# Five loads of x, statistics ahead of the first search, and another constant under the unread products, in a two-layer graph-and-expert kernel

## The chip, the cores and the metric

The kernel runs on one core of a Trainium2 chip, as one program launched once. The metric is the device time of that program in microseconds (us). Engines are named as in the profile: PE (matrix products; PEld is its weight loads), DVE (vector), ACT (scalar, activations), POOL (general), SP (here it only issues transfers). All five run their own instructions in order and wait for each other by semaphores. A name with a q behind it (SPq, ACTq, POOLq) is an engine's issue of DMA transfers.

## The reference

Two layers, each a graph step and an expert step, on x of 2708 x 256 in float32. Only the first layer's front is touched by the change:

```python
# layer 0, graph step: adj holds values up to 1e9, so each row's softmax is decided by its largest entry
h = layernorm(x) @ weight
logits = h @ conv_weight1 + (h @ conv_weight2).T
coefs = softmax(leaky_relu(logits) + adj, axis=-1)
x = x + coefs @ h + bias
# layer 0, expert step: layernorm, rmsnorm, causal attention with rotary positions, router, 8 experts, top 2
x = x + ffn0(layernorm(x))
# layer 1
x = x + sigmoid(masked_softmax_attention(layernorm(x), adj != 0))
x = x + ffn1(layernorm(x))
```

## The kernel before

The 2708 rows are 22 tiles of 128 rows (the last has 20). The function `first` does layer 0 up to the attention and the first experts' blocks. It doesn't multiply by the softmax: for each row it searches the adjacency's row for its largest entry (`top`, a MAX8, L974), finds where it is (`index`, L978), and fetches that row of h from memory with an indirect transfer that adds it into x (`fetch`, L996). The safety of that (the gap between the two largest entries and so on) is tested at the end by a flag.

**The planner.** `first` does not write its instructions in a fixed order. Each piece of work is a step given to a `Plan` (L74 to L146) with an engine, an assumed length in us, the steps it needs, buffers that it takes and gives back, a rank (lower goes first), and for a transfer a time `lands` between its issue and its data. `issue` plays this through on paper: at each turn it takes, of the steps that can start soonest, the one of the lowest rank, and emits its instructions. The emitted order is what each engine then runs. So the order is fixed when the program is built, from assumed lengths, and on the chip an engine whose next instruction is not ready waits, whatever stands behind it. Where the plan has a gap of over 1 us on PE, `fill` puts products nobody reads into it (0.75 x gap / 0.24 of them; each is two matmul records in the profile), which multiply the constant `allones` with the constant `before` (L1267).

**The steps around the change**, in the order in which a tile goes through them:

- the loads of x on SP: tiles 0 to 3, tiles 4 to 20, and the last tile (L834 to L839). Each has the rank -9; `lands` grows with the number of tiles.
- `rest` (ACT): transfers of the bias row, the routers and the second layer's graph weight; `wg_in`, a step without instructions, stands for the landing of the first layer's graph weight, whose transfer is issued before the plan starts (L184).
- `centre` (L866): PE multiplies the weight by ones to get column sums (L872), DVE takes the mean off (L876). It is done once for the graph weight (rank -3, result `wgc`) and once for the attention's `wq_sb` (rank -0.5), after `load_wq` (SP) and `order_wq` (ACT, L855 and L858).
- `project(t0)` for each pair of tiles, rank -1: `stats` (DVE, L267, L269, L897) and `power` (POOL, L901) give each row's scale; `turn` (PE, L908, rank -2) transposes x; `back` (ACT, L917) brings that from PSUM; `times` (PE, L928) multiplies by `wgc`, into one of two PSUM banks in turn; `out_` (ACT, L935) scales by `rsx` and frees the bank; `store` (ACT's queue, L940) writes the pair's h to `hd` in memory; `bias` (POOL, L912) adds the bias to x.
- `tile_in(t)` for each of the 22 tiles, rank t: `load` (SP, L969 the adjacency's 128 rows, 1354 KB, into one of three slots; L971 the rotary table), `top` and `index` (DVE, rank t + 2), `narrow` (ACT, L988, a bf16 copy of the adjacency in two halves; needs the last pair's `store`) and `save` (SP, L991), which frees the slot for tile t + 3; `fetch` (POOL, needs `index`, `bias` and every pair's `store`); then statistics, norm, transposes, the products for q, k, v and the rotary step.
- `pair(t0)`: the attention of two tiles of queries, on PE (L1100, L1126), ACT (L1106) and DVE (L1145), needs `tile_in` of all tiles up to t0 + 1.

Behind `first` follow the experts of layer 0, the second layer and its experts; all of it hangs on what is in front.

The constant `before` is made by POOL (an iota) and then by DVE (L231) in the preamble; `allones` by POOL alone (L228).

Of the kernel before, what the change touches and what calls it, by code (L numbers as in the profile page):

```python
# [17 lines left out]
PE, SP = mybir.EngineType.PE, mybir.EngineType.SP  # L18
PSUM = bass.MemoryType.PSUM

P = 128
N = 2708
C = 256
KC = C // P
NT = (N + P - 1) // P
# [40 lines left out]
def rows(t):  # L66
    return min(P, N - t * P)
# [6 lines left out]
class Plan:  # L74
# [16 lines left out]
    def add(self, engine, length, run, needs=(), take=(), give=(), rank=0.0, lands=0.0):  # L91
        step = dict(engine=engine, length=length, run=run, needs=[n for n in needs if n is not None],
                    take=take, give=give, rank=rank, lands=lands, end=None)
        self.steps.append(step)
        return step
# [54 lines left out]
def adj_ffn_kernel(ctx, tc, x, adj, vecs, bias_rows, tab, w_gnn0, w_gnn1, wqkv, wo,  # L150
                   r0, r1, w1_0, w3_0, w2_0, w1_1, w3_1, w2_1, out):
    nc = tc.nc
# [59 lines left out]
    def ramp(name, shape, pattern, base=0, mult=0):  # L212
        t = const.tile(shape, F32, name=name)
        nc.gpsimd.iota(t, pattern=pattern, base=base, channel_multiplier=mult,
                       allow_small_or_imprecise_dtypes=True)
        return t
# [10 lines left out]
    allones = const.tile([P, P], F32, name="allones")  # L227
    nc.gpsimd.memset(allones, 1.0)  # L228

    before = ramp("before", [P, P], [[1, P]], 0, -1)  # L230
# [34 lines left out]
    def moments(src, r):  # L265
        st = small.tile([P, nc.vector.BN_STATS_DIM], F32, tag="st", name="st")
        nc.vector.bn_stats(out=st[:r], in_=src)  # L267
        mv = small.tile([P, nc.vector.BN_AGGR_DIM], F32, tag="mv", name="mv")
        nc.vector.bn_aggr(out=mv[:r], in_=st[:r])  # L269
        return mv  # L270
# [517 lines left out]
    def first(X, XB, norms, tops, hd, mb, xs, acc, arena, load_weights):  # L788
# [11 lines left out]
        with ExitStack() as s:  # L800
# [29 lines left out]
            add = plan.add  # L830


            loads = []
            for a, b in ((0, 4), (4, NT - 1)):  # L834
                loads.append(add("SP", 0.5, lambda a=a, b=b: nc.sync.dma_start(
                    out=X[:, a:b, :], in_=x[a * P:b * P, :].rearrange("(t p) c -> p t c", p=P)),
                    rank=-9.0, lands=1.5 + 0.4 * (b - a)))
            loads.append(add("SP", 0.5, lambda: nc.sync.dma_start(
                out=X[:rows(NT - 1), NT - 1, :], in_=x[(NT - 1) * P:N, :]), rank=-9.0, lands=9.0))  # L839
            rest = add("ACT", 2.0, load_rest, rank=-9.0, lands=8.0)  # L840


# [17 lines left out]
            a = add("SP", 1.2, load_wq, loads, take=["e"], rank=1.5, lands=3.0)  # L860
# [5 lines left out]
            def centre(out_w, w, wide, needs, rank):  # L866
                v = {}

                def total():
                    v["p"] = mm_tile()  # L870
                    for k in range(KC):
                        nc.tensor.matmul(v["p"][:, :wide], allones, w[:, k, :], start=(k == 0), stop=(k == KC - 1))  # L872

                def less():
                    for k in range(KC):
                        nc.vector.scalar_tensor_tensor(out_w[:, k, :], v["p"][:, :wide], -1.0 / C, w[:, k, :],  # L876
                                                       ALU.mult, ALU.add)

                a = add("PE", wide / 256, total, needs, take=["mm"], rank=rank)
                return add("DVE", wide / 340, less, [a], give=["mm"], rank=rank)  # L880

            wg_in = add("SP", 0.0, lambda: None, rank=-9.0, lands=3.0)
            centred = centre(wgc, wg[0], C, [wg_in], -3.0), centre(wq_sb, wq_sb, 2 * C, [wq_in], -0.5)

            stored, biased = [], []
# [2 lines left out]
            def project(t0):  # L888
                two = [t0, t0 + 1]
                v = {}  # L890
                rank = -1.0
                bank = ("o", "zs")[t0 // 2 % 2]

                def stats(t):
                    r = rows(t)
                    v["mv", t], v["pv", t] = moments(X[:r, t, :], r), small.tile([P, 1], F32, tag="pv", name="pv")
                    nc.vector.tensor_scalar(v["pv", t][:r], v["mv", t][:r, 1:2], 1.0, 1e-5, ALU.mult, ALU.add)  # L897

                def power(t):
                    r = rows(t)  # L900
                    nc.gpsimd.tensor_tensor(out=rsx[:r, t:t + 1], in0=v["pv", t][:r], in1=mhalf[:r, 0:1], op=ALU.pow)  # L901

                def turn():
                    v["pt"] = tr_tile()
                    for i, t in enumerate(two):
                        r = rows(t)
                        for k in range(KC):
                            nc.tensor.transpose(v["pt"][:, i * KC + k, :r], X[:r, t, k * P:(k + 1) * P], ident[:r, :r])  # L908

                def bias(t):  # L910
                    r = rows(t)
                    nc.gpsimd.tensor_tensor(out=X[:r, t, :], in0=X[:r, t, :], in1=brow[:r, 0, :], op=ALU.add)  # L912

                def back():
                    v["xT"] = ab.tile([P, 2, NREP, P], F32, tag="yT", name="xTt").rearrange("p a b c -> p (a b) c")
                    if rows(t0 + 1) == P:
                        nc.scalar.copy(v["xT"], v["pt"])  # L917
                    else:
                        for i, t in enumerate(two):
                            nc.scalar.copy(v["xT"][:, i * KC:(i + 1) * KC, :rows(t)],  # L920
                                           v["pt"][:, i * KC:(i + 1) * KC, :rows(t)])

                def times():
                    v["po"] = afp.tile([P, 2 * W2], F32, tag=bank, name="po")
                    for i, t in enumerate(two):
                        r = rows(t)
                        for k in range(KC):
                            nc.tensor.matmul(v["po"][:r, i * C:(i + 1) * C], v["xT"][:, i * KC + k, :r], wgc[:, k, :],  # L928
                                             start=(k == 0), stop=(k == KC - 1))

                def out_():
                    v["hs"] = ab.tile([P, 2 * W2], F32, tag="osb", name="hs").rearrange("p (t c) -> p t c", t=2)
                    for i, t in enumerate(two):
                        r = rows(t)
                        nc.scalar.activation(v["hs"][:r, i, :], v["po"][:r, i * C:(i + 1) * C], AF.Copy,  # L935
                                             scale=rsx[:r, t:t + 1])

                def store():
                    if rows(t0 + 1) == P:
                        nc.scalar.dma_start(out=hd[t0 * P:(t0 + 2) * P, :].rearrange("(t p) c -> p t c", p=P),  # L940
                                            in_=v["hs"])
                    else:
                        for i, t in enumerate(two):
                            nc.scalar.dma_start(out=hd[t * P:t * P + rows(t), :], in_=v["hs"][:rows(t), i, :])

                x_in = [loads[0]] if t0 < 4 else [loads[1]] if t0 + 2 < NT else loads[1:]
                s_ = {t: add("DVE", 0.85, lambda t=t: stats(t), x_in, take=["mv"], rank=rank) for t in two}
                c = [add("POOL", 0.6, lambda t=t: power(t), [s_[t]], give=["mv"], rank=rank) for t in two]
                a = add("PE", 0.5, turn, x_in, take=["mm"], rank=rank - 1.0)
                for t in two:  # L950
                    biased.append(add("POOL", 0.8, lambda t=t: bias(t), [a, s_[t], rest], rank=rank + 1.5 + t / NT))
                a = add("ACT", 0.6, back, [a], take=["yT"], give=["mm"], rank=rank - 1.0)
                a = add("PE", 1.75, times, [a, centred[0]], take=[bank], give=["yT"], rank=rank)
                a = add("ACT", 0.95, out_, [a] + c, take=["ob"], give=[bank], rank=rank)
                stored.append(add("ACT", 0.35, store, [a], give=["ob"], rank=rank, lands=2.5))
# [285 lines left out]
            a = None  # L1241
            weights = []
            for e in range(2):
                a = add("SP", 6.0, lambda e=e: load_weights(e), cleared + [a], rank=NT + 3.0 + e, lands=3.0,
                        take=[] if e else [f"{a}{i}" for i in range(3) for a in ("adj", "low")])
# [17 lines left out]
            def idle(bank, pool):  # L1263
                def run(n):
                    nobody = pool.tile([P, 2 * W2], F32, tag=bank, name="nobody")
                    for _ in range(n):
                        nc.tensor.matmul(nobody[:, :P], allones, before, start=True, stop=True)  # L1267
                return run

            plan.fillers = [("zs", 1, idle("zs", afp)), ("o", 1, idle("o", afp))]  # L1270
# [1122 lines left out]
```

## Time and profile before

| what | us |
|---|---|
| three timed runs | 1506.54, 1506.64, 1509.68 (median 1506.64) |
| the profiled execution, its own time | 1506.29 |
| span of its records | 1504.5 |
| PE busy in the span | 1417.7 (94%) |
| DVE, ACT, POOL busy | 762.5, 567.4, 529.9 |
| third x load issued, then the first, second and third adjacency load | 5.51, 6.30, 9.61, 18.42 |
| first and last `times` begin (PE, L928; the last 8 of 16 records that run from 46.54 for 3.72) | 16.83, 48.4 |
| first `fetch` (POOL, L996) | 53.78 |
| fourth adjacency load issued | 57.28 |

The profile's page gives busy shares over the span, a strip of 40 slices, the costliest groups and the chain of waits that ended last. The trace behind it can be asked for the instructions of a stretch in order of time (a row is: start, duration, engine, line, operation, output tile and inputs, count, and in brackets how long the engine idled before and what released it) and for busy times in given stretches.

### The profile page before, as it was taken

The page shows a single profiled execution, that of the slowest core. Times are in us where ns is not written, and L with a number is a line of the kernel's source. Part 1 is how long each engine was busy: PE and PEld are TensorE (multiplying, and loading weights), DVE is VectorE, ACT ScalarE, POOL GpSimd, SP SyncE. Part 2 cuts the span into 40 slices and gives each one's busy share as a digit, 9 for nine tenths or more (in the row PEclk, how much of TensorE's full clock was granted, in tenths as well). Part 3 has the DMA queues.
Part 4 walks back from the last instruction along what each step waited for, and adds up shares of the span by engine and source line. Part 5 has one row for each costly group of instructions (what it writes and reads, how often), then busy time and mean ns, then how long its engine had stood idle before and what let it go on. Part 6 is the DMA issues. An engine that isn't in the chain of part 4 may idle for free. (4 is left out here: it accounts for less than half of the span.)

```text
span 1504.5 us, 21112 instructions
## 1 busy us (share of the span) xinstructions
PE 1417.7 (94%) x7488; PEld 1030.2 (68%) x7488; DVE 762.5 (51%) x1647; ACT 567.4 (38%) x1134; POOL 529.9 (35%) x681
## 2 busy tenths in 40 slices
PE   5878989989999999999999989999999999999995
PEld 5633433433335888888888778888769878888884
DVE  5688999966676322222222564766745322222221
ACT  2576776755554322222221443444323212122220
POOL 5577668782152221222222310030434122222222
PEclk9999999999999999999999999999999999999998
DMA  7599757430011666656411860633412965566111
GB/s 261 190 298 291 256 193 235 146 121 8 7 41 42 172 194 176 182 150 185 113 15 22 183 133 1 137 80 98 154 48 75 273 190 140 160 173 169 15 18 20
DMA packets 198519, 201.83 MB, mean 134 GB/s; under 512 B 93248, under 2 KB 168520, under 8 KB 195696
## 3 DMA queue, kind: packets, MB, share of 16 engines
q1 hardware_dynamic: 173782, 170.96, 37.4%
q0 software_dynamic: 20352, 25.85, 9.7%
q10 hardware_dynamic: 4270, 3.58, 0.7%
q8 instruction: 61, 1.00, 0.3%
q14 instruction: 54, 0.44, 0.1%
HBM read 128.46 MB, written 56.37 MB: 123 GB/s over the span
## 5 line engine op out<-in xcount | busy, mean ns | idle before, releaser
L2065 PE MATMUL pup<-xTs,arena 128*128 128x256 f32 (+2 forms) x1320 | 252.8, 350 | 0.6 <-ACT xTs L2048 0.6
L2065 PEld LDWEIGHTS pup<-xTs,arena 128*128 128x128 f32 (+1 forms) x1320 | 219.5, 190 | 28.3 <-PE y L2130 2.3
L1582 PE MATMUL po<-hb,PT 128*128 128x257 f32 (+2 forms) x968 | 228.5, 390 | 4.0 <-DVE PT L1575 4.0
L2069 ACT ACTIVATE sl<-pup 128x256 f32<-128x256 f32 (+1 forms) x210 | 73.6, 350 | 370.8 <-PE pup L2065 369.1
L1582 PEld LDWEIGHTS po<-hb,PT 128*128 128x128 f32 (+2 forms) x968 | 177.3, 189 | 44.0 <-issue 13.1
L2070 DVE TENSOR_TENSOR hT<-sl,pup 128x256 f32<-128x256 f32 (+1 forms) x210 | 79.6, 379 | 229.0 <-ACT sl L2069 228.7
L1106 ACT ACTIVATE e<-stt 128x1024 f32<-128x1024 f32 (+1 forms) x132 | 125.4, 986 | 93.6 <-PE stt L1100 68.5
L617 POOL DMA_INDIRECT out<-ys,XR x45 | 69.4, 1542 | 246.7 <-DVE ys L2083 110.0
L1145 DVE TENSOR_TENSOR es<-es,e 128x1024 f32<-128x1024 f32 x104 | 138.0, 1327 | 29.8 <-ACT e L1106 23.1
L617 POOL DMA_INDIRECT acc<-ys,XR x45 | 69.8, 1552 | 226.3 <-DVE ys L2083 94.5
L1100 PE MATMUL stt<-qT,kT 64*128 64x512 f32 (+1 forms) x528 | 132.6, 612 | 6.3 <-ACT e L1106 6.1
L2080 PE MATMUL y<-arena,hT 128*128 128x256 f32 x612 | 136.7, 379 | 0.0
L1809 POOL DMA_INDIRECT xs<-XR,place x88 | 93.4, 1061 | 92.8 <-DVE mk L1569 41.3
L2080 PEld LDWEIGHTS y<-arena,hT 128*128 128x128 f32 x612 | 114.3, 190 | 14.5
L1126 PE MATMUL o<-e,V 128*64 128x512 f32 (+1 forms) x528 | 123.3, 590 | 0.0
L1560 ACT ACTIVATE E<-sb,dcol 128x768 f32<-128x768 f32 (+1 forms) x88 | 75.1, 859 | 108.5 <-DVE PT L1575 108.2
L2083 DVE TENSOR_SCALAR ys<-y,XR 128x256 f32<-128x256 f32 x71 | 34.3, 484 | 141.2 <-PE y L2080 141.1
L2065 PE MATMUL pup<-xTs,room 128*128 128x256 f32 (+3 forms) x528 | 99.9, 346 | 0.0
L1100 PEld LDWEIGHTS stt<-qT,kT 64*128 64x128 f32 x528 | 44.4, 187 | 78.1 <-issue 61.7
L2065 PEld LDWEIGHTS pup<-xTs,room 128*128 128x128 f32 (+1 forms) x528 | 85.4, 189 | 9.8 <-PE y L2130 0.8
L1126 PEld LDWEIGHTS o<-e,V 128*64 128x64 f32 x528 | 33.2, 137 | 69.9 <-issue 55.4
L974 DVE MAX8 tops<-arena 128x8 f32<-128x2708 f32 (+1 forms) x22 | 65.3, 2970 | 1.8 <-DMA arena<-in_adj 1.8
(316 smaller groups left out, 2026.0 us busy)
## 6 DMA issues: line engine op xcount, KB each, us to landing
more<-in_w SPq DMA_DIRECT2D x60, 640.0 KB
arena<-in_adj SPq DMA_DIRECT2D x21, 1354.0 KB
arena<-in_w SPq DMA_DIRECT2D x36, 640.0 KB
mb<-mb SPq DMA_DIRECT2D x44, 352.0 KB
XR<-xs SPq DMA_DIRECT2D x80, 134.0 KB
xs<-none SPq DMA_DIRECT2D x16, 536.0 KB
room<-in_w SPq DMA_DIRECT2D x12, 640.0 KB
acc<-X SPq DMA_DIRECT2D x21, 128.0 KB
```

The costliest lines, as they stand in the source:

```text
L617: nc.gpsimd.indirect_dma_start(out=acc[:, :], out_offset=bass.IndirectOffsetOnAxis(ap=tokens.bitcast(I32), axis=0), in_=ys, in_offset=None ...
L1100: nc.tensor.matmul(st[:r, g, c0(sb):], kT[a:b, sb * P:sb * P + r], qT[a:b, t0 + (sb == t0 + 1):t0 + 2, :, :], start=True, stop=True)
L1106: nc.scalar.activation(e[:r, :, c0(sb):], v[sb, "st"][:r, :, c0(sb):], AF.Exp, scale=1.0 / HD ** 0.5)
L1126: nc.tensor.matmul(v["o"][g * HD:(g + 1) * HD, c:], V[:r, sb, g * HD:(g + 1) * HD], v[sb][:r, g, c:], start=(n + i == 0), stop=(n + i == t ...
L1145: nc.vector.tensor_tensor(es, es, v[sb][:r, :, c:], ALU.add)
L1560: nc.scalar.activation(e[:q, :n], sb[:q, i0:i1], AF.Exp, bias=dcol[:q, j:j + 1], scale=SLOPE - 1.0)
L1582: nc.tensor.matmul(v["po", i][:r, :F], v["PT", j][:q, a:a + r], hb[:q, j, :], start=(j == 0), stop=(j == NT - 1))
L1809: i = nc.gpsimd.indirect_dma_start(out=xs[:, :], out_offset=bass.IndirectOffsetOnAxis(ap=at, axis=0), in_=src, in_offset=None)
L2065: nc.tensor.matmul(pp[:to, i, :B, :], wn[:, c, :], xT[:, c, :B, :], start=(c == 0), stop=(c == KC - 1))
L2069: nc.scalar.activation(sl[:, :B, :], pp[:, 0, :B, :], AF.Silu)
L2070: nc.vector.tensor_tensor(hT[:, n, :B, :], sl[:, :B, :], pp[:, 1, :B, :], ALU.mult)
L2080: nc.tensor.matmul(y, hT[:, n, b, :], w[3][:, n, :], start=(n == 0), stop=(n == NHC - 1))
```

## The change

- x is loaded by six transfers in place of three: tiles 0 to 3, 4 to 7, 8 to 11, 12 to 15, 16 to 20, and the last. The planner's assumed time on SP is 0.55 us a tile (it was 0.5 us a transfer), and each lands 2.2 us later.
- `stats` of a tile and `turn` of a pair need the piece that holds them, where tiles 4 to 20 had one load for all.
- `turn` of every pair from the third on needs the centred weight `wgc`.
- `wg_in` becomes a step of ACT with rank -10 (it was on SP) and lands at 4.0.
- The unread products multiply `allones` with itself in place of `before`.

```diff
             loads = []
-            for a, b in ((0, 4), (4, NT - 1)):
-                loads.append(add("SP", 0.5, lambda a=a, b=b: nc.sync.dma_start(
+            ends = (4, 8, 12, 16, NT - 1, NT)
+            for a, b in zip((0,) + ends, ends[:-1]):
+                loads.append(add("SP", 0.55 * (b - a), lambda a=a, b=b: nc.sync.dma_start(
                     out=X[:, a:b, :], in_=x[a * P:b * P, :].rearrange("(t p) c -> p t c", p=P)),
-                    rank=-9.0, lands=1.5 + 0.4 * (b - a)))
-            loads.append(add("SP", 0.5, lambda: nc.sync.dma_start(
-                out=X[:rows(NT - 1), NT - 1, :], in_=x[(NT - 1) * P:N, :]), rank=-9.0, lands=9.0))
+                    rank=-9.0, lands=2.2))
+            loads.append(add("SP", 0.3, lambda: nc.sync.dma_start(
+                out=X[:rows(NT - 1), NT - 1, :], in_=x[(NT - 1) * P:N, :]), rank=-9.0, lands=2.2))
...
-            wg_in = add("SP", 0.0, lambda: None, rank=-9.0, lands=3.0)
+            wg_in = add("ACT", 0.0, lambda: None, rank=-10.0, lands=4.0)
...
-                x_in = [loads[0]] if t0 < 4 else [loads[1]] if t0 + 2 < NT else loads[1:]
-                s_ = {t: add("DVE", 0.85, lambda t=t: stats(t), x_in, take=["mv"], rank=rank) for t in two}
+                x_in = [loads[sum(t >= e for e in ends)] for t in two]
+                s_ = {t: add("DVE", 0.85, lambda t=t: stats(t), x_in[t - t0:t - t0 + 1], take=["mv"], rank=rank) for t in two}
                 c = [add("POOL", 0.6, lambda t=t: power(t), [s_[t]], give=["mv"], rank=rank) for t in two]
-                a = add("PE", 0.5, turn, x_in, take=["mm"], rank=rank - 1.0)
+
+                a = add("PE", 0.5, turn, x_in + [centred[0]] * (t0 > 2), take=["mm"], rank=rank - 1.0)
...
-                        nc.tensor.matmul(nobody[:, :P], allones, before, start=True, stop=True)
+                        nc.tensor.matmul(nobody[:, :P], allones, allones, start=True, stop=True)
```

## The prediction

> **What bounds the kernel now.** The page's own chain of waits covers the last 17 us alone, so I went by stages: first the busy times in stretches, then the instructions of the first 70 us in order of time, then SP's waits behind that. The stretches (us, PE, PEld, DVE, ACT, POOL busy, PE's granted clock, DMA share, GB/s):
>
> ```profile
> 0.00:57.00 57.00, 40.33 (x205) 34.29 (x206) 36.61 (x98) 21.38 (x45) 33.04 (x73) 0.91 0.60 204
> 57.00:160.00 103.00, 84.49 (x393) 40.64 (x393) 85.98 (x86) 73.04 (x134) 73.98 (x109) 0.97 0.88 286
> 160.00:310.00 150.00, 136.68 (x616) 58.55 (x617) 144.41 (x169) 104.11 (x182) 109.89 (x137) 0.99 0.65 210
> ...
> 15.00:27.00 12.00, 11.09 (x66) 9.72 (x65) 8.48 (x25) 3.41 (x8) 5.84 (x11) 1.00 1.03 360
> 27.00:55.00 28.00, 21.89 (x100) 17.46 (x101) 21.58 (x45) 14.01 (x34) 18.88 (x31) 0.85 0.30 107
> ```
>
> From 57 us on the tile loop keeps DVE and the transfers nearly full, then DVE and PE. Before it lies a prologue in which nothing is full, and from 27 to 55 us the transfers are at 0.30: three adjacency slots are loaded and the fourth waits. Why, the order of time shows:
>
> ```profile
> 9.14 0.22 DVE L231 TENSOR_SCALAR before<-before 128x128 f32<-128x128 f32 x1
> 9.41 4.22 PE L1267 MATMUL nobody<-before,allones 128*128 128x128 f32 x22 [9.41 <-DVE before L231]
> 13.47 1.04 PE L908 MATMUL pm<-ident,X 128*128 128x128 f32 x8
> 14.74 1.13 PE L872 MATMUL pm<-wg,allones 128*128 128x256 f32 x4 [0.24 <-ACT xTt L917]
> ...
> 16.83 1.89 PE L928 MATMUL po<-wgc,xTt 128*128 128x256 f32 x8
> ...
> 18.43 2.98 DVE L974 MAX8 tops<-arena 128x8 f32<-128x2708 f32 x1 [1.76 <-DMA arena<-in_adj]
> ...
> 21.33 0.41 DVE L267 BATCH_NORM_STATS2 st<-X 128x6 f32<-128x256 f32 x1
> ...
> 30.98 0.84 ACT L935 ACTIVATE hs<-po,rsx 128x256 f32<-128x256 f32 x2 [6.87 <-POOL rsx L901]
> ...
> 31.87 3.78 PE L928 MATMUL po<-wgc,xTt 128*128 128x256 f32 x8 [5.78 <-ACT hs L935]
> ```
>
> ```profile
> 50.85 0.99 ACTq L944 DMA_DIRECT2D hd<-hs  x2
> ...
> 53.78 1.79 POOL L996 DMA_INDIRECT X<-hd,ix  x1 [8.32 <-issue]
> ...
> 54.24 2.55 ACT L988 CAST mb<-arena 128x1408 bf16<-128x1408 f32 x2
> ...
> 57.28 0.41 SPq L969 DMA_DIRECT2D arena<-in_adj  x1
> ```
>
> Three things are to be seen. PE's first work (x's tiles 0 to 3 are in at 5.74, when the first statistics start) stands behind 22 unread records that wait for `before`, which DVE makes only after four tiles' statistics. DVE then sits in front of the first search until that adjacency tile lands (18.43), with the statistics of tiles 4 to 21 queued behind it; so a bank stays full and PE stands still from 26.1 to 31.87, and comes back at half rate (3.78 us for what takes 1.89). And the last store of h (50.85) releases the first fetch, the first narrowing and, through it, the fourth load: everything later hangs on the end of the projections.
>
> **The change, part by part.**
>
> Unread products on `allones`: POOL has that at 2.60 (a memset of 0.20 from 2.40). The plan's first PE step is now the centring, at 4.0 + 0.2; 4.2 x 0.75 / 0.24 is 13 products, 26 records. Before, 16 records took 3.39 us (9.41 to 12.80) and the last 6 took 0.83, so 26 end 3.39 + 10 x 0.138 = 4.77 later, at 7.4. The centring (1.13) ends at 8.55, its DVE half (15.91 to 16.66, 0.75) at 9.35. That releases the second `turn`'s buffer; two more transposes of 0.5 and `times` begins at about 10.6 instead of 16.83: **-6.2**. Bounds: if PE must wait as long as before for something unseen, 0; if the weight (SP's third load waited 3.6 us, to 5.5, for it) lets no product delay it, -8.
>
> Statistics first: in the plan the first adjacency load now starts at 11.85 (five pieces and the last, 2.2 x 4 + 2.75 + 0.3) and lands at 19.15; the statistics, 22 x 0.85 and the centring's 0.75 from 4.6, run until 24 and outrank it. On the chip a tile's statistics come every 0.81 us (21.33 to 22.13): tile 0 at 5.74, tile 1 at 9.35 behind the centring, tile 21 done at about 26.4. A pair takes PE 2.16 us (21.59 to 23.76), two tiles' statistics 1.62, so scales stay ahead. The pair that began at 31.87 begins 2.16 after its predecessor (25.93): **-5.9**. With no pause its half rate goes and the next, at 36.30, comes 2.16 later and not 4.43: **-2.3**. Bounds for the two together: -8.2, or half of it if POOL (per tile 0.54 of power and 0.72 of bias, 2.5 us a pair against PE's 2.16) falls behind with the scales; I take the whole, since the plan puts one bias behind about three powers, as in the rows from 23.6 to 31.6, where the statistics still kept 0.81.
>
> `order_wq` (four ACT instructions of 0.5) now falls into the steady run, where ACT waits 0.84 us a pair: 0 to +2, I take **+0.6**. The search that is moved back costs nothing while the last store is later than the first two indexes: six searches of 3.0 from 26.4, with 1.3 for `wq`'s centring and 0.4 for a small fold, end at 46.1, while the third index, at 57.02 before, would be due at 43.2. It is 2.9 late, or 7.2 late if DVE has tile 0's second statistics ahead of it. In front of the fourth search (67.87) DVE idled 3.31 + 3.21 + 0.78 = 7.3, which covers either; without the cover it costs 2.9 to 7.2. I take **+0.8**.
>
> Six x issues, SP: three more transfers in front of the first adjacency load, about 0.5 of SP each (rows of 0.46 to 0.74); and SP waits before an issue for older transfers (to 7.44, 9.61 and 15.03 in this trace). The first adjacency load moves from 6.30 to about 10.5, at worst 15.03, and lands between 18.43 and 27.2; DVE asks at 26.4: 0 to +0.8, I take 0, as the transfers ran full (1.0 and over) from 5 to 27 us whoever was first. The load of `wq` stands behind two adjacency loads on SP as before (15.40); at worst it too goes 8.7 later and its 2.7 MB of forerunners take 7.5 at 360 GB/s: 32 against ACT's turn at 29, +3 at most, taken as 0. The wait for `wgc` in `turn` and the move of `wg_in` add no instruction; their effect is the order above. A first piece of 512 KB is as before.
>
> One rule speaks against pieces. The Trainium skill, DMA: Bandwidth & Descriptors, section "Anatomy of one DMA — SWDGE (gpsimd) path", fits one transfer as 2.0 us plus its bytes at 436 GB/s (for POOL's own transfers; here SP issues). Estimated by that page, one after the other, pieces of 3.2, 3.2, 3.2, 3.2 and 3.5 bring tile 16 16.3 us after the first issue, at 17.1. By the rows x as a whole was in by 15.03, where SP's wait of 5.1 for one of its loads ended, and tile 16's statistics come at 9.35 + 15 x 0.81 = 21.5. So the sum is the same by both.
>
> **Sum:** -6.2 - 5.9 - 2.3 + 0.6 + 0.8 = -13.0. The first fetch moves from 53.78 to about 40, the fourth load from 57.28 to 43.5. What follows only hangs on that, in the same order as far as I can tell. The profiled execution took 1506.29 (span 1504.5), 0.35 under the median of the runs; 1506.64 - 13.0 = **1493.6**.
>
> **Rivals.**
>
> *Half is given back in the tile loop.* The loop's pace is its own (DVE 0.83 and transfers 0.88 busy from 57 to 160), and a third tile late by 7.2 without cover leaves 13 + 0.8 - 7.2 = 6.6: 1500.0. For: DVE's order is in the planner's hands. Against: the idle rows above.
>
> *It doesn't do what it says.* If PE is held at the start as before by another wait, and the pause only moves (a late `wq` on ACT, POOL's scales), what is left is 4.1 of the 8.2, less 2 for `order_wq`, less 3 for `wq`: 0.9 lost, 1507.5, no change.
>
> *Slower: the loads behind narrowing.* A new order in the loop can put `narrow` behind more exponentials on ACT. SP stands in its save with the next adjacency load behind it:
>
> ```profile
> SPq L991 <- ACT mb L988: 57.1, 20, 6.9
> ```
>
> That is 57.1 us in 20 waits from 57 to 160, the longest 6.9; from 160 to 300 the longest is 10.9. It decides once new waits exceed 13 us; the two longest once more, 17.8, give 1493.6 + 17.8 = 1511. For: all three engines of the loop run an order made on paper. Against: ranks and costs of the loop are untouched.
>
> **How the numbers follow.** The forecast has 0.63, the half 0.14, no change 0.08, slower 0.15. I predict the likeliest, 1493.5. Its own range is 1490 to 1500: the best ends of the terms are -8 - 8.2 = -16.2, and above it reaches to the half; all worst ends at once (-4.1 + 2 + 7.2 + 0.8 + 3) would be a loss, which the other cases hold. The whole range, 1486 to 1507, leaves out most of the slower case, and below it allows 4 us for a loop that happens to be ordered better. About 0.2%, 3 us, is what a measurement of this kernel can tell from no change. So faster 0.77, same 0.08, slower 0.15.
>
> **What would show it.** Unread products from 2.6; `times` first at 10 to 11; no pause of PE over 3 us and no half-rate `times` before the last store; 22 statistics in a row, then the first search at 26 to 27; first fetch at 38 to 42, fourth load 41 to 46; at 160 us the same work 10 to 14 us earlier. Wrong if ACT waits for `wq`, if x's later pieces stop the statistics, or if tiles 3 to 21 are searched more than 3 us further apart in sum.

## The result, and the profile after

The changed kernel took 1507.57 us in the median of 18 runs (1501.38 to 1512.0), the kernel before 1506.57 in 18 runs beside them: ratio 1.0005, 95% interval 0.999 to 1.0019. That is no change; the forecast was 1493.5, with a range from 1486 to 1507. The profiled execution's span is 1506.0 (1504.5 before).

The busy times of the changed kernel in the stretches shown of before (us, PE, PEld, DVE, ACT, POOL, granted clock, DMA share, GB/s):

```profile
0.00:57.00 57.00, 45.30 (x234) 36.89 (x235) 37.76 (x101) 24.88 (x49) 34.92 (x77) 0.94 0.69 234
57.00:160.00 103.00, 87.19 (x402) 41.22 (x400) 88.08 (x83) 72.71 (x133) 74.02 (x108) 0.93 0.85 281
160.00:310.00 150.00, 133.27 (x568) 55.47 (x568) 136.16 (x162) 101.74 (x174) 98.75 (x127) 0.95 0.54 179
```

```profile
15.00:27.00 12.00, 8.16 (x34) 6.07 (x32) 10.06 (x44) 2.43 (x6) 11.05 (x21) 0.86 1.03 383
27.00:55.00 28.00, 23.42 (x128) 18.99 (x128) 17.72 (x14) 15.92 (x34) 15.58 (x22) 0.94 0.41 135
```

Up to 57 us PE has done 5.0 us more work than before, unread products counted. From 160 to 310 it does 3.4 less and DVE 8.3 less, and the transfers fall from 0.65 to 0.54: what the front won is gone there. The front in order of time, rows of PE, DVE, ACT and POOL picked from the timeline (start, duration, engine, line, operation, count, idle before it and its releaser):

```profile
2.65 4.71 PE L1269 MATMUL nobody<-allones 128*128 128x128 f32 x26 [2.65 <-POOL allones L228]
7.20 1.03 PE L873 MATMUL pm<-wg,allones 128*128 128x256 f32 x4
...
10.00 1.89 PE L929 MATMUL po<-wgc,xTt 128*128 128x256 f32 x8
...
18.63 0.37 ACTq L941 DMA_DIRECT2D hd<-hs  x1
19.05 0.58 ACT L918 COPY xTt<-pm 128x512 f32<-128x512 f32 x1 [3.62 <-DMA tb<-in_tab]
...
21.53 0.84 ACT L936 ACTIVATE hs<-po,rsx 128x256 f32<-128x256 f32 x2 [1.90 <-POOL X L913]
...
22.42 3.26 PE L929 MATMUL po<-wgc,xTt 128*128 128x256 f32 x8 [2.08 <-ACT hs L936]
...
26.42 2.97 DVE L976 MAX8 tops<-arena 128x8 f32<-128x2708 f32 x1
...
28.31 0.84 ACT L936 ACTIVATE hs<-po,rsx 128x256 f32<-128x256 f32 x2 [4.63 <-DMA hd<-hs]
...
29.20 3.23 PE L929 MATMUL po<-wgc,xTt 128*128 128x256 f32 x8 [2.67 <-ACT hs L936]
...
45.03 0.99 ACTq L945 DMA_DIRECT2D hd<-hs  x2
...
47.82 1.79 POOL L998 DMA_INDIRECT X<-hd,ix  x1 [11.07 <-DMA hd<-hs]
```

The start is as forecast: unread products at 2.65, first `times` at 10.00, the first search at 26.42. But PE has two pauses instead of one, and comes back slower after each (3.26 and 3.23 us for what takes 1.89). Both come from ACT, which waits in `store` for a completion semaphore (the counter that a transfer raises when it has landed) that the rotary table's load used last, and in `out_` for an older store of h. That holds for the first pause too, though its row names POOL: by the trace's semaphore updates the store issued at 13.35 had landed at 21.45, and `out_` begins at 21.53. The first fetch is 6.0 us earlier (47.82 against 53.78), not 14. The last products of the attention into `o`, a landmark that every run has, begin at 472.98 against 470.77: 2.2 later. From 390 us on the order of work is the same in both; behind the landmark the offset wanders between 0.1 and 2.5.

So two questions: why the front won 6 instead of 14, and where the loop lost it again (8.2 between these two executions).

### The profile page after: what moved, and what is told of

It reads as the page before. It is cut to its first block, busy times and chain, and to the rows that moved or that the text cites. A ratio compares the mean times of both kernels' runs of the same rounds, so it can differ in the third digit from the quotient of the medians.

```text
span 1506.0 us, 21081 instructions
## 1 busy us (share of the span) xinstructions
PE 1421.2 (94%) x7478; PEld 1028.7 (68%) x7478; DVE 761.7 (51%) x1647; ACT 569.7 (38%) x1134; POOL 523.6 (35%) x681
## 5 line engine op out<-in xcount | busy, mean ns | idle before, releaser
L1147 DVE TENSOR_TENSOR es<-es,e 128x1024 f32<-128x1024 f32 x104 | 134.5, 1293 | 30.6 <-ACT e L1108 22.7
L1128 PE MATMUL o<-e,V 128*64 128x512 f32 (+1 forms) x528 | 126.6, 604 | 0.0
L980 DVE FIND_INDEX8 ix<-tops,arena 128x8 uint32<-128x2708 f32 (+1 forms) x22 | 65.4, 2971 | 0.0
```

The lines of the kernel that those rows point to most:

```text
L1128: nc.tensor.matmul(v["o"][g * HD:(g + 1) * HD, c:], V[:r, sb, g * HD:(g + 1) * HD], v[sb][:r, g, c:], start=(n + i == 0), stop=(n + i == t ...
L1147: nc.vector.tensor_tensor(es, es, v[sb][:r, :, c:], ALU.add)
```

## The experiments

All ratios are to the kernel before, run beside on the same chip. "Fetch" is the first fetch's start, "last" the landmark; both are read from one profiled execution. The expectations call PE TensorE, DVE VectorE, ACT ScalarE and POOL GpSimd. Executions of one and the same front differ by up to 3.5 us: the changed kernel's has its fetch at 47.82, 48.96 (e1, with one bias addition more), 45.45 (e5) and 45.43 (e13), that of before at 53.78, 52.11 (e2) and 51.74 (e14). The landmark varies as much: e3 below, with the order and the time of the kernel before, has it 2.9 later. So smaller differences in either are not read, and where a landmark and a ratio disagree, the ratio counts, since it is of all runs.

**Order and front exchanged.** A function that emits the steps in a written list (left out here) replaces the planner's choice in `first`:

```diff
-                plan.issue()
+                follow(plan, ORDER)
```

e1: the changed kernel, up to the first fetch in its own order, then in the order of before. 

> The changed kernel, but the order of the work is written out: up to the first fetch as the changed kernel's planner made it, behind it as the planner of the kernel before made it. Theory A (the new order of the tile loop gives back what the front gained): the first fetch is at 48 as in the changed kernel (53.8 before), the lead of 6 us lasts through the attention, its last product (before: 470.8, changed: 473.0) is at 464 to 466, and the time is 1500 to 1502. Theory B (the loop runs at its own pace, and an earlier start is lost in it whatever the order): the last product at 470 to 472, the time 1506 to 1508.


Measured: 0.9972 (0.9956 to 0.9988), fetch 48.96, last 464.80, as theory A had it.

e2: the kernel before with the order of the changed kernel's loop. 

> The kernel before, with the order written out: up to the first fetch as its own planner made it, behind it as the changed kernel's planner made it. Theory A: the first fetch at 54, and the loop's new order costs 6 to 9 us: last product of the attention at 477 to 480, time 1512 to 1516. Theory B: last product at 471 to 473, time 1506 to 1508.


Measured: 1.0034 (1.0018 to 1.005), fetch 52.11, last 475.08. Theory A again, at a smaller price. The loop's new order costs 8.2 us at the landmark with the one front and 4.3 with the other; by the ratios it is 5.0 (1.0005 against 0.9972) and 5.1.

**The constant by itself.**

```diff
-                        nc.tensor.matmul(nobody[:, :P], allones, before, start=True, stop=True)
+                        nc.tensor.matmul(nobody[:, :P], allones, allones, start=True, stop=True)
```

e3: this on the kernel before, and the same in the second layer's unread products (L1668), which the change leaves alone. 

> The kernel before with the other constant under the unread products and nothing else; the order is untouched. If the start of PE sets the end of the projections: first products 6 us earlier, first fetch at 48, time 1500. If the statistics behind the first search set it (so I think now): PE's first transposes at about 7 instead of 13.4, its pause that ended at 31.87 is longer and ends at the same time, first fetch at 53 to 54, time 1506 to 1507.


Measured: 0.9992 (0.9975 to 1.001), fetch 51.39, last 473.72.

e4: the changed kernel with this line undone. 

> The changed kernel with the old constant under the unread products; the order is untouched. They start at about 6.9 instead of 2.65 and PE's first useful work is 4 us later. If ACT's waits for transfers (to 19.05, 23.1 and 28.3 in the changed kernel's trace) set the end of the projections: first fetch at 47.5 to 49, time as the changed kernel's, 1506 to 1509. If PE's start sets it: first fetch at 52, time 1510 to 1512.


Measured: 1.0029 (1.0013 to 1.0046), fetch 51.40, last 478.07. The earlier start of PE shows no gain alone; within the change, as the second alternative had it, the fetch comes 2.4 to 6.0 us earlier with it, by the four executions above.

**One place of the loop's order.** The trace of the changed kernel has VectorE stand still twice at 167 to 172 us (DVE rows of the timeline):

```profile
161.43 4.69 DVE L1147 TENSOR_TENSOR es<-es,e 128x1024 f32<-128x1024 f32 x4
166.04 0.16 DVE L394 TENSOR_SCALAR meansq<-meansq 128x6 f32<-128x6 f32 x1
167.34 0.43 DVE L267 BATCH_NORM_STATS2 st<-X 128x6 f32<-128x256 f32 x1 [1.14 <-DMA X<-hd,ix]
...
172.09 0.43 DVE L267 BATCH_NORM_STATS2 st<-X 128x6 f32<-128x256 f32 x1 [3.85 <-DMA X<-hd,ix]
...
172.91 2.55 DVE L1147 TENSOR_TENSOR es<-es,e 128x1024 f32<-128x1024 f32 x2
175.38 2.98 DVE L976 MAX8 tops<-arena 128x8 f32<-128x2708 f32 x1
```

and PE behind it:

```profile
175.61 1.08 PE L1180 MATMUL pm<-es,allones 128*64 128x512 f32 x4 [4.16 <-DVE es L1147]
...
179.37 3.68 PE L1128 MATMUL o<-e,V 128*64 128x512 f32 x8
```

The fetches of tiles 12 and 13 were issued at 160.50 and 162.53; their statistics stand in front of work that was ready, a sum and the search of tile 14. e5 exchanges these steps (the list has numbers; here they are in words):

```diff
-statistics(12) statistics(13) sums power(13) top(14)
+statistics(12) top(14) sums statistics(13) power(13)
```

> The changed kernel with one place of its order altered: on VectorE the statistics of tile 13 (and their power on GpSimd) stand behind the first search of tile 14 and the exponentials' sum beside it, as they stand in the order that follows the kernel before; all else as in the changed kernel, where VectorE stood still 1.1 + 3.9 us at 167 to 172 us for fetched rows and TensorE then ran 8 products in 3.7 instead of 1.9 us. Theory A (the loop's order gives the front's gain back, and this is the place that costs most): the two idle times shrink to under 1.5 us together, the last o product of the attention comes at 467 to 470 (472.98 in the changed kernel, 464.80 with the whole order of before), and the time is 1501 to 1504 on the scale where the changed kernel has 1507.6 (ratio to before 0.9965 to 0.9985). Rival R1 (no single place; the order costs a little everywhere): the idle time moves to the next statistics, the last product stays within 1.5 us of 473, ratio 0.9995 to 1.0025.


Measured: 0.995 (0.993 to 0.997), fetch 45.45, last 462.93. Its VectorE in the same place:

```profile
165.92 0.43 DVE L267 BATCH_NORM_STATS2 st<-X 128x6 f32<-128x256 f32 x1 [1.39 <-DMA X<-hd,ix]
...
166.74 2.97 DVE L976 MAX8 tops<-arena 128x8 f32<-128x2708 f32 x1
169.64 2.53 DVE L1147 TENSOR_TENSOR es<-es,e 128x1024 f32<-128x1024 f32 x2
172.09 0.42 DVE L267 BATCH_NORM_STATS2 st<-X 128x6 f32<-128x256 f32 x1
```

The gain is larger than either theory's. The 3.85 are gone. The landmark moved by 10.0, of which 1.7 were there before this place (index of tile 12 at 148.68 against 150.35). The 8.4 left are more than the hole: the lead over the changed kernel is 4.3 at the index of tile 14 and 8.4 at that of tile 19. This one exchange at 160 us is worth 0.55% (0.995 against 1.0005), more than the 0.33% between the changed kernel and e1.

**The front's stores.** `out_` has two buffers for `hs`, so it waits for the store two pairs before. More of them are to be had from the exponentials' pool, of which only one buffer, for the raw wqkv, is in use then:

```diff
-                    v["hs"] = ab.tile([P, 2 * W2], F32, tag="osb", name="hs").rearrange("p (t c) -> p t c", t=2)
+                    if t0 // 2 % 2:
+                        hs = abe.tile([P, NKV, 2 * W2], F32, tag="e", name="hs")[:, 0, :]
+                    else:
+                        hs = ab.tile([P, 2 * W2], F32, tag="osb", name="hs")
+                    v["hs"] = hs.rearrange("p (t c) -> p t c", t=2)
```

e7a: this on the changed kernel, all orders as there. 

> The changed kernel with one alteration: every second pair's scaled product goes to a buffer of the exponentials' pool, which is unused then, so that a store of hd has four pairs of time instead of two before its buffer is wanted again. Order of all steps as in the changed kernel. Theory A: of the two long waits on ScalarE the one for a store's landing (4.63 us at 23.7 to 28.3) goes, the other (3.62 us behind the rotary table's semaphore) stays or moves, the first fetch comes at 43 to 46 (47.8), the last store at 40 to 43 (45.0). Theory that the shared completion semaphore is all: no change of the first fetch beyond 1 us. The loop's order is still the changed kernel's, so the last o product is expected at 468 to 472 and the ratio at 0.996 to 1.000.


Measured: 0.9928 (0.99 to 0.9957), fetch 38.13, last 463.49. ScalarE's waits in the front (us in all, times, longest), and rows of its PE:

```profile
ACT hs L940 <- DMA hd<-hs: 0.2, 1, 0.2
```

```profile
10.78 1.89 PE L929 MATMUL po<-wgc,xTt 128*128 128x256 f32 x8
...
19.45 1.89 PE L929 MATMUL po<-wgc,xTt 128*128 128x256 f32 x8
...
28.21 3.72 PE L929 MATMUL po<-wgc,xTt 128*128 128x256 f32 x16
```

The products now run through at 2.17 a pair, full rate, and the fetch comes where the prediction had it (38 to 42). The wait behind the rotary table, expected to stay, went too: the compiler dealt the semaphores anew, and the second store now shares one with a piece of x instead of the table. What each of the two was worth was not separated.

e7b: also wqkv and wo, the second and the third adjacency load issued behind the third, fifth and ninth store. 

> As the run with more buffers, and besides the loads of wqkv and wo, of the second and of the third adjacency tile are issued in that order behind the third, fifth and ninth store of hd, so that no store waits on a semaphore of a load that lies behind an adjacency tile. Engines' order otherwise that of the changed kernel. Theory A: both long waits on ScalarE go (each under 0.8 us), the products run through at 2.2 us a pair, the last store is issued at 36 to 40, the first fetch at 40 to 43, VectorE's wait for wqkv's centring shrinks from 10.2 us to under 5, the last o product at 464 to 469, ratio 0.993 to 0.998. If instead TensorE's own pace sets the front (half rate after every pause), the last store comes no earlier than 41 and the first fetch no earlier than 44.


Measured: 0.994 (0.9919 to 0.996), fetch 39.20, last 461.48. Nothing beyond e7a.

e6: a front like e7b's, with five bias additions and wqkv's centring later, and before's order of the loop. 

> The changed kernel with the order of the loop of before (as in e1) and with the front's waits taken away: the stores of hd go out of four and more buffers instead of two, the second and third adjacency tile are issued behind some of the stores, the order, centring of wqkv and its VectorE part come behind the last product of the front, and five bias additions behind the first two fetches. Theory A, front's part (ScalarE waited for slow stores and for a completion semaphore shared with a load, the rest hung on that): the products of the front run through from 10.0 at 2.2 us a pair, the last store of hd is issued at 34 to 38 (45.0 in the changed kernel, 50.9 before), the first fetch at 38 to 42 (47.8 and 53.8), the last o product at 455 to 460 (464.8 in e1), ratio to before 0.989 to 0.994. Rival R2 (the tile loop has its own bound, VectorE's searches or the adjacency's loads, which a front earlier by another 8 us does not move): first fetch as above, but last product 462 to 466 and ratio 0.996 to 0.999. Rival R3 (the stores are slow because adjacency rows hold the DMA engines, so buffers only move the wait to the last store's landing): last store issued early, first fetch still at 46 or later.


Measured: 0.9937 (0.9915 to 0.9959), fetch 38.47, last 464.08. The fetch is 10.5 earlier than in e1, the landmark 0.7, but the ratio is 0.35% lower (5.3 us; the intervals touch). So the ratio lies in theory A's range and the landmark in rival R2's, and this run does not decide between them. The order is that of e1, instruction for instruction behind the front; from 40 to 160 us VectorE waits 16.6 us for fetched rows (11.1 in e1). With a front this early before's order is no better than the changed kernel's own (0.9928 in e7a). So e1 hadn't shown that before's order is the better one, only that it suited that front.

e8: e7a's buffers and e5's exchange. 

> The two edits that were each faster, together: more buffers for the front's stores (first fetch at 38.1 instead of 47.8) and the statistics of tile 13 behind the first search of tile 14 (last o product 462.9 with it, 463.5 with the buffers). Theory A (two separate losses of the changed kernel, one in the front and one at 160 to 180 us, so they add): last o product at 454 to 458, ratio to before 0.986 to 0.990. Rival R2 (the tile loop has a bound of its own, as the run with the mended front and the order of before suggests, where 10.5 us of lead came out as 0.7): last product 460 to 464, ratio 0.991 to 0.995.


Measured: 0.9903 (0.9881 to 0.9924), last 457.03. The two losses are separate; they add in the main (16 us at the landmark, of 10.0 and 9.5 alone).

e10: the buffers on the kernel before, nothing of the change. 

> The kernel before with the additional buffers for the front's stores alone. There the statistics behind the first search set the front, by the prediction's reading, so the stores' buffers should be worth nothing: first fetch at 52 to 54.5, last o product at 469 to 473, ratio 0.998 to 1.002. If the stores' landing set the front before as well: first fetch under 49, ratio under 0.997.


Measured: 0.9964 (0.9948 to 0.9981), fetch 46.53, last 466.21. The second alternative, against the prediction's reading, and the most telling result. The statistics behind the search are where they were, and yet the pause of PE is gone; `out_` of the third pair, held until 30.98 before, runs here at 24.79:

```profile
22.63 0.85 ACT L939 ACTIVATE hs<-po,rsx 128x256 f32<-128x256 f32 x2
23.50 0.37 ACTq L944 DMA_DIRECT2D hd<-hs  x1
24.31 0.59 ACT L917 COPY xTt<-pm 128x512 f32<-128x512 f32 x1 [0.84 <-PE po L928]
24.79 0.84 ACT L939 ACTIVATE hs<-po,rsx 128x256 f32<-128x256 f32 x2
```

**What the planner is told.** On paper a fetch lands 2.5 us after an issue of 1.6, so 4.1 us after the issue's start. In the changed kernel the rows of the two fetches above let their statistics start 6.8 and 9.6 us after it.

```diff
-                a = add("POOL", 1.6, fetch, [a, biased[t]] + stored, give=["ix"], rank=rank, lands=2.5)
+                a = add("POOL", 1.6, fetch, [a, biased[t]] + stored, give=["ix"], rank=rank, lands=7.0)
```

e9: this and the buffers on the changed kernel. 

> The changed kernel with more buffers, and the planner told that a fetch lands 7.0 us after its issue instead of 2.5 (6.5 to 9.6 us in the traces so far); the planner then makes its own order. If the loop loses by an order planned for fetches that land too soon: VectorE's waits for fetched rows at 40 to 310 us fall from 23 us to under 12, the last o product comes at 450 to 459 and the ratio at 0.982 to 0.990. If the planner's order is a draw from a lottery whatever it is told: the waits may fall, but the last product lies anywhere from 458 to 475, ratio 0.991 to 1.003.


Measured: 0.9882 (0.9858 to 0.9907), 1486.92 us, fetch 38.67, last 453.48. VectorE's waits for rows from 40 to 310 us, first in the changed kernel (22.8 in e7a, which has this front), then here:

```profile
DVE st L267 <- DMA X<-hd,ix: 21.0, 9, 4.6
```

```profile
DVE st L267 <- DMA X<-hd,ix: 1.7, 2, 1.1
```

This is the fastest version, and beats both kernels.

e11: e8 with the statistics of tiles 2, 5, 6 and 8 moved behind a search or a reciprocal by hand as well. 

> As the run with both edits, and the statistics of tiles 2, 5, 6 and 8, which waited 3.7, 1.8, 2.0 and 5.1 us for their rows with the buffers, stand one or two searches or reciprocals later on VectorE. If an in-order VectorE that waits for rows is what the loop loses, nearly the sum comes out where VectorE is the bound: of 12.5 us some 5 to 10, last o product at 446 to 453, ratio 0.980 to 0.986. If the later statistics only make TensorE's products late in its place, or the adjacency's loads set the pace of the searches: within 3 us of the run with both edits.


Measured: 0.9916 (0.9887 to 0.9944), last 460.20. The second alternative, nearly (3.2 us behind e8's landmark): the waits for rows from 40 to 310 fall to 7.5 us, but others come (4.6 for adjacency loads, 4.4 and 3.4 for products and scales in front of the joins), and nothing is won. A wait taken away in one place is worth something only if what follows is ready.

e12: buffers and landing on the kernel before. 

> The kernel before with the additional buffers for the front's stores and the planner told 7.0 us for a fetch's landing; nothing of the change. If the change itself is worth its front (the first fetch at 38.7 with it and both mends, 46.5 without it and with the buffers), this comes 4 to 8 us later than the changed kernel with both mends: first fetch at 45 to 48, last o product at 457 to 462, ratio to before 0.991 to 0.994 (0.9882 there). If the change is worth nothing once both are mended (the tile loop being bound by VectorE's searches and the adjacency's loads): last o product at 452 to 455, ratio 0.987 to 0.990.


Measured: 0.9932 (0.9911 to 0.9954), fetch 45.66, last 459.68, the first alternative.

e13: the landing alone on the changed kernel. 

> The changed kernel with its two store buffers, and the planner told 7.0 us for a fetch's landing. Front as in the changed kernel: first fetch at 45 to 49. If the order's part of the loss is mended by the planned landing alone, VectorE's waits for fetched rows at 40 to 310 us stay under 6 us, the last o product comes at 460 to 466 and the ratio at 0.993 to 0.997. If the new order needs the earlier front to be worth anything: last o product at 467 or later, ratio 0.997 or more.


Measured: 0.9942 (0.9921 to 0.9963), fetch 45.43, last 461.59, waits for rows 2.7: the first alternative.

e14: the landing alone on the kernel before. 

> The kernel before with its two store buffers and nothing of the change, the planner told 7.0 us for a fetch's landing. First fetch at 51 to 54 as before. If the planned landing mends what VectorE loses in waits for rows (15.7 us at 60 to 310 in the kernel before): those waits fall under 5 us, last o product at 462 to 467, ratio 0.993 to 0.998, and the changed kernel with the same planning (0.9942) is then 0 to 4 us ahead. If the planned landing helps the changed kernel alone, because the order before was by luck a good one: ratio 0.998 to 1.002, last product 468 or later.


Measured: 0.9968 (0.9946 to 0.999), fetch 51.74, last 467.43, waits for rows 4.9: the first alternative.

The eight together, ratio and last product:

| | landing 2.5 | landing 7.0 |
|---|---|---|
| before, two buffers | 1, 470.8 | 0.9968, 467.4 |
| changed, two buffers | 1.0005, 473.0 | 0.9942, 461.6 |
| before, more buffers | 0.9964, 466.2 | 0.9932, 459.7 |
| changed, more buffers | 0.9928, 463.5 | 0.9882, 453.5 |

With both mended the change itself is worth 0.5%, and the intervals (0.9911 to 0.9954, 0.9858 to 0.9907) are apart; with one of them mended it is ahead too, but the intervals overlap, and alone it is worth nothing. The longer landing is faster in every row, clear of noise in the two rows with two buffers (the intervals of the other two overlap). It is one other value, and no order drawn at random was run beside it, so how much of a row's gain is a lucky order is not known.

## Why the prediction was wrong

**Unread products, -6.2: right.** First `times` at 10.00 instead of 16.83, -6.8.

**Pause and half rate, -5.9 and -2.3: the step that failed first.** It said that VectorE's statistics behind the first search kept a bank full. It took the row of `out_` at its word, "6.87 <-POOL rsx". That instruction is the third pair's, tiles 4 and 5. Their powers were done by 23.64, as these rows of the kernel before (POOL, ACT) show:

```profile
19.69 0.38 ACTq L940 DMA_DIRECT2D hd<-hs  x1
...
22.29 0.54 POOL L901 TENSOR_TENSOR rsx<-pv,mhalf 128x1 f32<-128x1 f32 x1 [5.58 <-DVE pv L897]
...
23.10 0.54 POOL L901 TENSOR_TENSOR rsx<-pv,mhalf 128x1 f32<-128x1 f32 x1 [0.27 <-DVE pv L897]
```

It ran 7.3 us later. It waits for two semaphores, POOL's and that of the store two pairs before, issued at 19.69; the name in the bracket was of a POOL record that ended near 30.9 but belonged to a much later tile. By the trace's semaphore updates that store landed in 16 parts, from 28.11 to 30.90, and `out_` begins at 30.98. e10 shows the same: its buffer out of the way, the fetch comes 7.2 us earlier with the order of all engines untouched. The sum's 8.2 was the right size for the pause and named the wrong owner. So moving the statistics could not remove it; the pause came back as the 4.63 for a store's landing, beside the 3.62 for the semaphore.

**Loads, `order_wq`, POOL:** x in pieces and the biases cost nothing that shows (the fifth piece had landed at 14.57, where the prediction's estimate for pieces one after the other was 17.1); the first search began at 26.42 (26 to 27 said). But `order_wq` ran at 41.58 and not in the steady run (29), and VectorE waited 10.18 us for wqkv's centring, until 45.53. That is the front's lateness again: with more buffers (e7a) its DVE half begins at 36.15 without a wait.

**"What follows only hangs on that, in the same order": the step that took the rest.** The planner makes the loop's order anew from every change of its front, and this draw had two fetched tiles' statistics ahead of ready work. The front's 6.0 passed on as 2.2 lost in these two executions; by the ratios the front was worth 4.2 us (e1) and the order took 5.0. e5 shows the place. e13 and e14 show that a planner told 7.0 us instead of 2.5 makes a faster order; that it is faster because DVE waits less for rows fits (2.7 and 4.9 us instead of 21.0 and 15.7) but is not shown by itself, since in e11 such waits went without a gain. The idle times that the prediction counted as cover in front of the fourth search (3.31, 3.21 and 0.78) were already waits of this kind.

**The rivals.** "Half is given back in the tile loop" had the right place and too small a price: all that the front had won went. "It doesn't do what it says" had the time (1507.5), but in part by luck: the first products did move; the pause did stay, for the stores and not for `wq` or POOL's scales; the rest went in the loop, which it left alone. The slower rival, a new order with the adjacency's loads behind narrowing, came with a longer wait in the saves (longest 17.6 us from 160 to 300, 10.9 before), but that did not decide: e5 leaves one of 15.0 and is 0.55% faster than the changed kernel.

That the order, and not a pace of the loop's own, held the changed kernel is shown by e5 and e13, which have its front and are faster. How much of a lead an order keeps differs: by the ratios 10.5 us at the fetch gave 5.3 in e1's order (e6), and 9.7 gave 11.6 in the changed kernel's (e7a), with wide intervals. What makes a given order keep a lead was not settled beyond VectorE's waits for rows.

## What to carry to other kernels

When an instruction waits for several semaphores, work out when each could have been met; if the one named was met long before, look for a transfer whose buffer is wanted again. Where a planner fixes the order from assumed durations, a changed front re-orders the rest: measure the assumed landings against the trace before judging the change, and judge it under an order that fits.

## What was not expected of the hardware

A store of 256 KB took 11.2 us in the kernel before from its issue (19.69) until it had landed (30.90, by the semaphore updates), while an adjacency load was under way (issued at 18.42, landed at 30.42; DMA share 1.03 from 15 to 27 us). The next one, issued at 22.71, took 8.8; the eight issued from 31.85 on, with no such load beside them, 2.1 to 2.3 each. In the changed kernel it is 7.5 to 9.6 beside loads, and 2.1 to 2.4 from 29.18 on, as the last of these loads ends (29.52). The Trainium skill, DMA: Bandwidth & Descriptors, section "Queues, rings and completion order", says that each DMA engine takes turns between queue rows a whole packet at a time; that would fit a store of 1 KB rows beside adjacency rows of 10.8 KB on another queue, but no run here isolates it.

A fetch of 128 rows of 1 KB was ready 6.8 and 9.6 us after the start of its issue; in the kernel before the profile has the landing 3.9 to 9.2 us after it, with a median of 6.6. The same page's section "Anatomy of one DMA — SWDGE (gpsimd) path" would make it 2.3 us by its fit (an estimate: 2.0 and 131 KB at 436 GB/s). The measurement decides here; the planner's 4.1 was near the fastest of them.

ACT stood 3.6 us in front of a copy that doesn't read the rotary table, until that table's load was complete: the store ahead of it shared a completion semaphore with a load that another engine had issued behind 1354 KB (issued at 8.98, landed at 18.56; the store was issued at 18.63).
